# A four-direction scan layer: 32x32 tiles for gates, input and output products, gathered in one block per pair

## The chip, the core and the metric

The kernel runs on one core of a Trainium2 chip. The metric is the device time of one execution in microseconds (us), the median of several runs; lower is better. The core has five engines that run side by side and wait for each other by semaphores: PE (TensorE, matmuls; its weight loads are listed as PEld), DVE (VectorE), ACT (ScalarE), POOL (GpSimd) and SP (SyncE, here the queue that issues DMAs). [...] 

[...] All data are float32, and each float32 matmul of the program appears in the profile as two passes (two MATMUL records with a weight load each), so the profile has 24,090 records for 12,047 products.

## What is computed

The input x is (4, 128, 96, 96). It is normalized over groups of 4 channels (32 groups), run through the same layer in four scan orders (by rows, by rows backwards, by columns, by columns backwards), the four results are joined by a 1x1 product (fuse), and x is added.

```python
t = _grouped1x1(x, in_proj_w, in_proj_b, G)          # 128 -> 512 channels, 4 groups of 32
u, gate = (t[:, :HID], t[:, HID:])                   # HID = 256
u = jax.nn.silu(u)
u = conv_general_dilated(u, dw_w, ...)               # 5 taps, one filter per channel
s = _conv1x1(u, ssm_in_w)                            # 256 -> 32
a = DMIN + (DMAX - DMIN) * sigmoid(_conv1x1(u, ssm_delta_w, ssm_delta_b))
bb = tanh(_conv1x1(u, ssm_b_w, ssm_b_b)); cc = tanh(_conv1x1(u, ssm_c_w, ssm_c_b))
hst = scan of h = a * h + bb * s                     # written with cumsums in the reference
u = u + _conv1x1(cc * hst + ssm_d[None, :, None] * s, ssm_out_w)
u = _grouped1x1(u * sigmoid(gate), mix_w, mix_b, G)
return _conv1x1(u, out_proj_w, out_proj_b)
```

## The kernel before

**Tiling.** A batch element has two phases, V (columns) and H (rows); each phase treats its forward and backward order together (s = 0 and 1). A phase has NS = 6 steps of 16 lines, a step has R = 4 pairs; pair t holds the two units 2t (s = 0) and 2t + 1 (s = 1), each N = 384 positions wide (every fourth position of the step). That makes 8 phases, NP = 24 pairs a phase, 192 pairs in all; k = t % 4 is the place in the step. Because the backward order of one half of the lines is the forward order of the other, only the first three steps of a phase are computed up to the activations ("fresh"); the rest reads them mirrored, kept in DRAM meanwhile (`kept_sil`, and `kept` for gates). Gates belong to pair n = t - LAG (LAG = 6): the pair t works on the convolution and projection of its own units and, six pairs behind, on gate, output and final product of pair n. `mirror(n)` is None for the first 12 of 24, whose gates are computed.

**One pair.** The order on every engine is that of the program text (a manual schedule); `pair(t)` writes it out:
- in_proj of group g for the step after (`front`, L407 to L484; only while that step is fresh, t % 24 in 20 to 23 and 0 to 7): 16 products of 32x32 into four banks, then four silus on ACT (L470).
- the convolution of the first 128 channels on PE: `conv` (8 products, 128 x 32, "band") and `conv_less` (8 products, 64 x 32, "less", row half changing with s, column with g), copied to `u` by ACT (L629, L631). The other 128 channels on DVE: `first_tap` on ACT (L648), four taps on DVE (L650), in banks 0 and 1.
- W, the final product of two units gated in the pair before (`accumulate`, L742; 16 products, 128 x 32, "w_fin", to two banks), copied by ACT to `ys` (L755, L757) and added to `acc` by POOL (L774).
- `under` (L509): ACT seeds the output banks (0 and 1 for s = 0, 2 and 3 for s = 1) with u, so that the output product adds to it.
- gates (`gate`, L487; four products of 32x128, for pairs whose gates are computed) and outputs (`out_of`, L501; four products of 32x128), tanh of the gates on ACT (L521), and `gating` on DVE (L597), which multiplies.
- `proj` (L662): 16 products, 128 x 32, weights "main", to two banks; ACT evacuates them (L687, L688, L693), POOL forms decay and input of the scan (L695, L696).
- for k < 2 half of the scan of the step before on DVE (L722), and `outputs` on POOL (L728 to L731), which need it and feed the output product of a later pair.

The pairs differ: 10 of 24 have in_proj and outputs, 10 gates and outputs, two all three (t % 24 = 6, 7), two outputs alone (18, 19). PSUM banks 4 to 7 serve conv, W, in_proj, gates and proj in turn (`plan`, `GATE`, L121 to L127). The group norm of the next batch element is made in pieces (`stats_finish`, a generator; each `yield` ends a piece) between the pairs.

Of the kernel before, what the change touches and what calls it, by code (L numbers as in the profile page):

```python
# [67 lines left out]
def conv_preact_kernel(  # L68
# [111 lines left out]
    def stats_finish(b):  # L180

        mv = sp.tile([P, 2], F32, tag="mv", name=f"mv_{b}")
# [5 lines left out]
        nc.vector.tensor_copy(mean, pm[:, 0:1])  # L193
        dev = sp.tile([P, 1], F32, tag="dev", name=f"dev_{b}")
# [12 lines left out]
        nc.vector.tensor_scalar_add(var, pv[:, 0:2], GN_EPS)  # L207
        inv = sp.tile([P, 2], F32, tag="inv", name=f"inv_{b}")
        if b == b0:
            std = sp.tile([P, 2], F32, tag="err", name="std")  # L210
            nc.scalar.activation(std, var, AF.Sqrt)

            nc.scalar.activation(first_table, std[:, 0:1], AF.Silu)
            nc.vector.reciprocal(inv, std)
        else:
            bits = inv.bitcast(I32)
            nc.vector.tensor_single_scalar(bits, var.bitcast(I32), 1, ALU.logical_shift_right)
            nc.vector.tensor_scalar(bits, bits, -1.0, float(0x5F3759DF), ALU.mult, ALU.add)
            err = sp.tile([P, 2], F32, tag="err", name=f"err_{b}")
            for turn in range(3):  # L220
                if turn:
                    yield
                nc.gpsimd.tensor_mul(err, inv, inv)
# [3 lines left out]
        yield  # L227
        wns = sp.tile([P, 2, P], F32, tag="wn", name=f"wn_{b}")
        for e in range(2):
            nc.vector.tensor_scalar_mul(wns[:, e, :], w_in[:, e, :], inv[:, e : e + 1])  # L230
        wn = wns[:, 0, :]

        bn = sp.tile([P, 8], F32, tag="bnorm", name=f"bnorm_{b}")
        stats[b] = (wns, bn)
        yield


        pb = bank(free[0])
        product(pb[:, 0:4], wn, gm4)
        if b == b0:  # L240
            for g in range(4):
                for q in range(R):
                    mm(pb[:, 4 + g : 5 + g], q, wn[0:32, 32 * g : 32 * g + 32], mean[0:32, :], True, True)
            nc.vector.tensor_sub(bn, b_in, pb[:, 0:8])
        else:
            nc.vector.tensor_sub(bn[:, 0:4], b_in[:, 0:4], pb[:, 0:4])
            spread = sp.tile([P, 4], F32, tag="spread", name=f"spread_{b}")
            shift = sp.tile([P, 1], F32, tag="shift", name=f"shift_{b}")
            nc.vector.tensor_copy(shift, pb[:, 0:1])
            nc.vector.tensor_scalar_mul(spread, gmask, shift)  # L250
# [4 lines left out]
            nc.vector.tensor_sub(bn[:, 4:8], b_in[:, 4:8], pq[:, 0:4])  # L255
        nc.vector.tensor_scalar_mul(bn[:, 2:4], bn[:, 2:4], 0.5)


# [35 lines left out]
    def load_x(chunks):  # L294
        for c, n in chunks:
            nc.sync.dma_start(accf[:, bass.ds(c * SC, n * SC)], xr[b0, :, bass.ds(c * SC, n * SC)])  # L296
            for e in range(c, c + n):
                nc.vector.bn_stats(stats_of(b0)[:, e, :], accf[:, bass.ts(e, SC)])

    b0 = phases[0][0]  # L300
    mid = wp.tile([P, 1], F32, name="mid")
    nc.gpsimd.memset(mid, MID)
# [5 lines left out]
    w_out_fuse = load(fuse, "fuse")  # L308
    w_main = load(main, "main")
    for s in range(2):  # L310
        load_front(0, s, half(s), slice(0, R))
# [8 lines left out]
    w_mix = w_out_fuse[:, HID + 4 * P :].rearrange("p (j c) -> p j c", j=2)  # L320
    w_in, w_proj = (
        w_main[:, bass.ts(e, HID)].rearrange("p (j c) -> p j c", j=2) for e in range(2)
    )
# [135 lines left out]
            )  # L459

    def in_proj(step, g, s, j, bk):
        wn = stats[units[step * UB]["b"]][0]
        r = slice(64 * s + 32 * j, 64 * s + 32 * j + 32)
        for c in range(4):
            m, q = (c, g) if j else (g, R - 1 - c if s else c)
            mm(bank(bk), c, wn[r, s, 32 * m : 32 * m + 32], x_in[s][r, q, :], True, True)

    def silu(step, g, s, j, bk):
        bn = stats[units[step * UB]["b"]][1]
        nc.scalar.activation(  # L470
            sils[step][:, s, j, g, :],
            bank(bk)[:, : N + 1],
            AF.Silu,
            bias=bn[:, 1:2] if j else bn[:, 4 + g : 5 + g],
        )
# [11 lines left out]
    def gate(bi, s, j, to):  # L487
# [3 lines left out]
        nc.tensor.matmul(bank(to)[:, :N], stats[un["b"]][0][r, s, :], x_in[s][r, q, off : off + N],  # L491
                         start=True, stop=True)

    turning = (6, 0, 2)

    def ssm(bi, s):
# [4 lines left out]
    def out_of(bi, s, j):  # L501
# [2 lines left out]
        nc.tensor.matmul(bank(ssm(bi, s) + j)[:, :N], w_so[r, bass.ts(j, P)], z[r, :],  # L504
                         start=bi not in seeded, stop=True, skip_group_check=True)

    seeded = set()

    def under(bi, s):  # L509

        seeded.add(bi)
        nc.scalar.copy(psum[:, ssm(bi, s) : ssm(bi, s) + 2, :N], us[bi][:, s])  # L512

    def sigmoids(bi, to):
        bn = stats[units[bi]["b"]][1]
# [66 lines left out]
    def gating(bi, s):  # L582
# [1 line left out]
        v = units[bi + s]["v"] = us[bi][:, s]  # L584
        m = mirror(bi // 2)
        if m is None:
            g = gates[bi // 2 % 2][:, s]
        else:
            g = old_gates.get(bi // 2, gates[m % 2])[:, 1 - s, :, ::-1]
# [29 lines left out]
    def conv_less(i, banks):  # L619
# [7 lines left out]
        if banks == PROJ:  # L627
            for s in range(2):
                nc.scalar.copy(us[i][:, s, 0, :], bank(b0 + s)[:, :N])  # L629
# [167 lines left out]
    def pair(t):  # L797
# [124 lines left out]
        if bi > 0 and bi % (NU // B) == 0:  # L922
            send()

    def tail():

        first, end = NU // 2 - LAG, NU // 2
# [86 lines left out]
                nc.sync.dma_start(out[bu["b"], :, region], accf[:, region])  # L1014

    def start():
        w_of = wp.tile([P, 4, 2, P], F32, name="w_of")
# [93 lines left out]
    with tc.manual_schedule(  # L1111
# [2 lines left out]
        }  # L1114
    ):
        start()
        for t in range(NU // 2):
            pair(t)
        tail()


# [79 lines left out]
```

## Time and profile before

| what | us |
|---|---|
| three timed runs | 1810.45, 1811.15, 1817.87 |
| their median | 1811.15 |
| profiled execution, span from first to last instruction (its own time; none beside the span is listed) | 1812.7 |
| from the projection of pair 7 to that of pair 191 (184 pairs) | 1689.8 |

The profile names, for each engine, its busy time in the span, the chain of work that ended last (followed back from the last instruction to what released each step), groups of equal instructions with their mean duration, what each engine waited for, and the instructions in order of time. A row such as "914.09 0.88 PE L134 MATMUL psum<-sil,less 64*32 64x384 f32 x16" reads: from 914.09 us on, for 0.88 us, PE ran 16 passes of line 134, which read tiles sil and less with weights of 64 rows and 32 columns, and wrote to PSUM. "[0.16 <-PE psum L134]" behind a row is the time the engine stood idle before it, and whose end released it. L134 is the helper `mm`, so its rows are told apart by their tiles. PE's busy time overlaps itself, as matmuls are pipelined; the time from the start of one group to the start of the next is what a group takes.

### The profile page before, as it was taken

What the parts mean: (1) busy time and instruction counts of PE and PEld (TensorE: products, weight loads), DVE (VectorE), ACT (ScalarE), POOL (GpSimd) and SP (SyncE); (2) the same over time, 40 slices, a digit from 0 to 9 for tenths busy, and PEclk for the clock granted to TensorE, in tenths of its full rate; (3) what the DMA queues carried; (4) which work ended last, traced back from release to release, by engine and by line L of the source; (5) the groups of instructions that cost most, each with busy time, mean ns of one, the idle gap of its engine ahead of it and who ended that gap; (6) DMA issues with size and microseconds to landing.
All of it is one profiled execution on the core that took longest, in us unless ns stands there. A gap on an engine that the chain in (4) does not pass through costs nothing.

```text
span 1812.7 us, 56970 instructions
## 1 busy us (share of the span) xinstructions
PE 1788.9 (99%) x24090; PEld 645.3 (36%) x24090; DVE 1446.5 (80%) x1462; ACT 1567.0 (86%) x2750; POOL 1432.0 (79%) x1477
## 2 busy tenths in 40 slices
PE   6999999999999999999999999999999999999998
PEld 3333333333333333333333333333333333333333
DVE  5888878887888887877788888787877878777886
ACT  4988888998888888898988888889888888889975
POOL 3587887778778888788877888778778788887876
PEclk9999999999999999999999999999999999999999
DMA  7655463444975466344696447443477734645434
GB/s 229 183 184 196 149 185 117 163 145 142 305 246 188 159 177 204 102 145 141 204 306 225 159 161 211 138 146 119 160 232 223 249 118 150 192 122 176 148 112 175
DMA packets 148047, 321.17 MB, mean 177 GB/s; under 512 B 14160, under 2 KB 115920, under 8 KB 147792
## 3 DMA queue, kind: packets, MB, share of 16 engines
q1 hardware_dynamic: 147648, 317.48, 54.4%
q8 instruction: 190, 3.11, 0.7%
q14 instruction: 65, 0.53, 0.1%
q10 hardware_dynamic: 144, 0.04, 0.0%
HBM read 185.21 MB, written 132.25 MB: 175 GB/s over the span
## 4 chain that ended last, share of the span: by engine, by line
PE 95%; DMA 2%; DVE 2%; ACT 1%; issue 0%; SPq 0%; DVEq 0%
PE psum L134 82%; PE psum L504 8%; PE psum L491 5%; DVE psum L650 1%; DMA x_in<-in_xs 1%; DMA xs<-in_xr 1%; DMA acc<-in_xr 0%; DVE u L597 0%; DVE u L650 0%; ACT psum L512 0%; PE psum L1035 0%; ACT u L631 0%; SPq L296 0%; ACT ys L757 0%; DVE bn L387 0%
## 5 line engine op out<-in xcount | busy, mean ns | idle before, releaser
L650 DVE SCALAR_TENSOR_TENSOR psum<-sil,small,psum 128x768 f32<-128x768 f32 x576 | 589.0, 1023 | 28.4 <-ACT psum L648 3.4
L597 DVE SCALAR_TENSOR_TENSOR u<-gate,psum 128x768 f32<-128x768 f32 x376 | 350.0, 953 | 273.4 <-ACT u L629 119.0
L134 PE MATMUL psum<-u,w_fin 128*32 128x384 f32 (+1 forms) x6192 | 551.1, 485 | 1.6 <-ACT ys L755 1.2
L134 PE MATMUL psum<-u,main 128*32 128x384 f32 x6144 | 534.7, 489 | 1.5 <-DVE u L650 1.4
L774 POOL TENSOR_TENSOR acc<-ys,acc 128x384 f32<-128x384 f32 x375 | 411.6, 1119 | 24.0 <-ACT ys L757 7.9
L728 POOL TENSOR_TENSOR t<-t,t 64x384 f32<-64x384 f32 (+1 forms) x192 | 237.7, 1238 | 156.9 <-DVE t L722 73.2
L134 PEld LDWEIGHTS psum<-u,w_fin 128*32 128x32 f32 x6192 | 189.3, 109 | 319.6 <-issue 215.3
L134 PEld LDWEIGHTS psum<-u,main 128*32 128x32 f32 x6144 | 181.9, 109 | 324.7 <-issue 197.2
L512 ACT COPY psum<-u 128x768 f32<-128x768 f32 x352 | 277.3, 801 | 17.5 <-DVE u L650 11.5
L134 PE MATMUL psum<-sil,band 128*32 128x384 f32 x3072 | 285.1, 488 | 0.0
L695 POOL TENSOR_SCALAR t<-tm 64x384 f32<-64x384 f32 x191 | 176.9, 926 | 117.3 <-ACT tm L687 97.9
L729 POOL TENSOR_TENSOR t<-t,t 64x384 f32<-64x384 f32 (+1 forms) x192 | 249.1, 1297 | 15.0
L504 PE MATMUL psum<-t,main 32*128 32x384 f32 x1536 | 238.6, 513 | 1.3 <-ACT psum L512 0.6
L648 ACT ACTIVATE psum<-sil,small 128x768 f32<-128x768 f32 x191 | 173.7, 909 | 56.2 <-DVE u L597 48.0
L521 ACT ACTIVATE gate<-psum,bnorm 128x384 f32<-128x384 f32 x384 | 192.2, 584 | 26.5 <-PE psum L491 25.5
L696 POOL TENSOR_TENSOR t<-t,tm 64x384 f32<-64x384 f32 x192 | 195.3, 1017 | 15.3
L650 DVE SCALAR_TENSOR_TENSOR u<-sil,small,psum 128x768 f32<-128x768 f32 x192 | 194.9, 1015 | 7.8
L470 ACT ACTIVATE sil<-psum,bnorm 128x385 f32<-128x385 f32 x384 | 192.6, 585 | 7.1 <-PE psum L134 4.8
L134 PE MATMUL psum<-sil,less 64*32 64x384 f32 x3072 | 168.1, 495 | 0.0
L491 PE MATMUL psum<-x_in,wn 32*128 32x384 f32 x768 | 157.3, 527 | 0.0
L134 PEld LDWEIGHTS psum<-sil,band 128*32 128x32 f32 x3072 | 90.6, 109 | 169.2 <-issue 94.4
L731 POOL COPY t<-t 64x384 f32<-64x384 f32 x187 | 136.8, 731 | 11.9
(103 smaller groups left out, 1480.3 us busy)
## 6 DMA issues: line engine op xcount, KB each, us to landing
sil<-sil SPq DMA_DIRECT2D x128, 770.0 KB, 6.7
kept<-gate SPq DMA_DIRECT2D x80, 768.0 KB, 3.7
gate<-kept SPq DMA_DIRECT2D x76, 768.0 KB, 4.9
x_in<-in_xs SPq DMA_DIRECT2D x192, 96.2 KB, 2.5
out<-acc SPq DMA_DIRECT2D x48, 384.0 KB, 8.2
acc<-in_xr SPq DMA_DIRECT2D x39, 384.0 KB, 6.8
xs<-in_xr SPq DMA_DIRECT2D x72, 192.0 KB, 5.7
x_in<-in_xs SPq DMA_DIRECT2D x46, 192.5 KB, 3.5
```

The source lines that it names most:

```text
L134: nc.tensor.matmul(o[r, : rhs.shape[-1]], lhsT, rhs, start=start, stop=stop, skip_group_check=True)
L470: nc.scalar.activation(sils[step][:, s, j, g, :], bank(bk)[:, : N + 1], AF.Silu, bias=bn[:, 1:2] if j else bn[:, 4 + g : 5 + g],)
L491: nc.tensor.matmul(bank(to)[:, :N], stats[un["b"]][0][r, s, :], x_in[s][r, q, off : off + N], start=True, stop=True)
L504: nc.tensor.matmul(bank(ssm(bi, s) + j)[:, :N], w_so[r, bass.ts(j, P)], z[r, :], start=bi not in seeded, stop=True, skip_group_check=True)
L512: nc.scalar.copy(psum[:, ssm(bi, s) : ssm(bi, s) + 2, :N], us[bi][:, s])
L521: nc.scalar.activation(gv[:, s, j, :], bank(to[2 * s + j])[:, :N], AF.Tanh, bias=bn[:, 2 + j : 3 + j], scale=0.5,)
L597: nc.vector.scalar_tensor_tensor(v, g, 1.0, pz, ALU.add, ALU.mult)
L650: nc.vector.scalar_tensor_tensor(us[i][:, :, 1, :] if k == K - 1 else part, src, w_tap[:, k : k + 1], part, ALU.mult, ALU.add,)
L696: nc.gpsimd.tensor_mul(ta[0:64, p, :], tb[0:64, :], tm[0:64, :])
L728: engine.tensor_mul(ta[0:64, p, r], tb[64:P, r], ta[64:P, p, r])
L729: engine.tensor_add(tb[0:64, r], ta[0:64, p, r], tb[0:64, r])
L774: adder.tensor_add(part, y, part)
```

## The change

The pairs from t = LAG + 2 = 8 on go to a new function, `pair_of_tiles`, instead of `pair`. In it:
- gates and output products are split into four products of 32x32 (`gate_tile`, `out_tile`); in_proj has that shape already. One block of 32 products per pair holds 16 output products and 16 others: in_proj in the pairs that had it; otherwise gates of the pair n + 1 (one pair ahead of their use); in t % 24 = 17, 18, 19, where neither is left, the gates of the first three pairs of the next phase, which go through one tile `shared` to DRAM and come back later. The row group runs fastest, then the column. The block comes in two halves (j = 1, then 0): the first writes banks `pb` and 0, 1, the second `ob` and 2, 3.
- silu and tanh of the first half are one per bank, those of the second half one over two banks.
- order on PE: for k > 1 W, conv, less, block, proj; for k < 2 conv, less, W, block, proj. in_proj, which stood first in the pair, now stands in the block behind them. For k > 1 one of the two conv copies is DVE's.
- banks 6, 7 and 4, 5 change places from pair to pair; both output banks are always seeded.
- `stats_finish` is cut into smaller pieces, two of which run in each pair with k > 1.
- the weights of the start (`w_out_fuse`, `w_of`) lie in the tile `shared`, which is free after the start.

In numbers of instructions in the program (PE: products): 12,047 become 15,383; gates and outputs of 32x128 fall from 384 and 768 to 8 and 32, those of 32x32 rise from 0 to 1,504 and 2,944. ACT: silus 384 become 216 and 84 over two banks, tanhs 384 become 194 and 95, seeds 352 become 380, conv copies 178 and 103 (two banks) become 102 and 95, with 92 on DVE. Additions of u on DVE (L596) fall from 32 to 4. Gate loads from DRAM rise from 76 to 97; gate stores stay 80.

```diff
+    def gate_tile(n, s, j, to, c):
+        un = units[2 * n + s]
+        q, off = gate_at(un)
+        r = slice(64 * (1 - s) + 32 * j, 64 * (1 - s) + 32 * j + 32)
+        mm(bank(to), c, stats[un["b"]][0][r, s, bass.ts(c, 32)], x_in[s][r, q, off : off + N],
+           True, True)
...
+    def out_tile(bi, s, j, c):
+        r = slice(64 * j + 32 * s, 64 * j + 32 * s + 32)
+        mm(bank(ssm(bi, s) + j), c, w_so[r, bass.ds(j * P + 32 * c, 32)], tbs[bi][r, :], False, True)
...
+    def tanh_both(n, to, j, b0):
+        bn = stats[units[2 * n]["b"]][1]
+        nc.scalar.activation(
+            to[:, :, j, :],
+            psum[:, b0 : b0 + 2, :N],
+            AF.Tanh,
+            bias=bn[:, 2 + j : 3 + j],
+            scale=0.5,
+        )
...
+    def tile_of(n):
+        m = mirror(n)
+        return gates[((n % NP if m is None else m) + n // NP) % 2]
+
     def load_kept(n):
         m = mirror(n)
+        if n % NP < 3 and NP <= n < NU // 2:
+            nc.sync.dma_start(tile_of(n), kept[n // NP % 2][n % NP])
         if n < NU // 2 - R and m is not None and m < NP // 2 - 2:
-            old_gates[n] = gates[m % 2]
-            nc.sync.dma_start(old_gates[n], kept[n // NP % 2][m])
+            nc.sync.dma_start(tile_of(n), kept[n // NP % 2][m])
...
+    def less_both(i, banks):
+        step, p = units[i]["step"], units[i]["p"]
+        sil, k = blocks(step), less_of(p)
+        for g in range(4):
+            for s in range(2):
+                r = less_rows(s, p)
+                mm(bank(banks[s]), g, less[r, p, g, :], columns(step, sil[s][r, g, :], k), False, True)
...
+    def pair_of_tiles(t):
+        i, k, n, end = 2 * t, t % R, t - LAG, NU // 2
+        bi, last = 2 * n, t == end - 1
+        w_first = k > 1
+        pb, ob = ((6, 7), (4, 5))[:: 1 if t % 2 == 0 else -1]
+        cb, db = (ob, pb) if w_first else (pb, ob)
...
+        if mirror(n + 1) is None and (n + 1) % NP > 2:
+            gated = n + 1
+            to = tile_of(gated)
+        elif t % NP in (17, 18, 19) and t + LAG + 1 < end:
+            gated = t + LAG + 1
+            to = shared()[:, : 4 * N].rearrange("p (s j n) -> p s j n", s=2, j=2)
...
+        if t == LAG + 2:
+            for j in (1, 0):
+                b0 = pb[0] if j else SSM + 2
+                for c in range(4):
+                    for s in range(2):
+                        gate_tile(n, s, j, b0 + s, c)
+                tanh_both(n, tile_of(n), j, b0)
...
+        taps(i, (1, 2))
+        piece = later and k > 1
+        if piece:
+            free[0] = SSM + 2
+            next(later[0], None)
+        taps(i, (3, 4))
+        if piece:
+            next(later[0], None)
...
+        def convolution():
+            conv(i, cb)
+            if w_first:
+                under(bi, 0)
+            less_both(i, cb)
+            if w_first:
+                stats_chunks(t)
+                nc.scalar.copy(us[i][:, 0, 0, :], bank(cb[0])[:, :N])
+                nc.vector.tensor_copy(us[i][:, 1, 0, :], bank(cb[1])[:, :N])
+            else:
+                nc.scalar.copy(us[i][:, :, 0, :], psum[:, cb[0] : cb[0] + 2, :N])
+                under(bi, 0)
+                stats_chunks(t)
+
+        under(bi, 1)
+        if t > LAG + 2:
+            scale_s(i - 4)
+        if k < 2:
+            scan(t // R - 1, k)
+        if k != 1:
+            outputs(i - 10)
+        for part in (products, convolution) if w_first else (convolution, products):
+            part()
+        if k == 1:
+            outputs(i - 10)
...
+        for j in (1, 0):
+            for c in range(4):
+                for s in range(2):
+                    if fronted:
+                        in_proj_tile(step, g, s, j, (ob, pb)[j][s], c)
+                    elif gated is not None:
+                        gate_tile(gated, s, j, (ob, pb)[j][s], c)
+                for e in range(2):
+                    out_tile(bi, 1 - j, e, c)
+
+        if fronted:
+            for s in range(2):
+                silu(step, g, s, 1, pb[s])
+        elif gated is not None:
+            for s in range(2):
+                tanh_one(gated, to, s, 1, pb[s])
+        gating(bi, 0)
+        first_tap(i + 2)
+        gating(bi, 1)
+        if fronted:
+            silu_both(step, g, 0, ob[0])
...
+        elif gated is not None:
+            tanh_both(gated, to, 0, ob[0])
+            if gated % NP < NP // 2 - 2:
+                nc.sync.dma_start(kept[gated // NP % 2][gated % NP], to)
+            for s in range(2):
+                load_gate(2 * gated + s + UB)
...
+        proj(i, pb, True)
...
         start()
-        for t in range(NU // 2):
+        for t in range(LAG + 2):
             pair(t)
+        for t in range(LAG + 2, NU // 2):
+            pair_of_tiles(t)
         tail()
```

More of the change, by code (lines that the diff above doesn't have):

```diff
@@ L298, in load_x, with shared @@
                 nc.vector.bn_stats(stats_of(b0)[:, e, :], accf[:, bass.ts(e, SC)])
+    rp = ctx.enter_context(tc.tile_pool(name="shared", bufs=1))
+    def shared():
+        return rp.tile([P, 16 * P], F32, tag="shared", name="shared")
     b0 = phases[0][0]
@@ L307, in conv_preact_kernel @@
     load_x([(0, 1), (1, 1), (2, 1), (3, 2), (5, 2), (7, 3), (10, 4), (14, 4), (18, 4), (22, 2)])
-    w_out_fuse = load(fuse, "fuse")
+    w_out_fuse = shared()
+    nc.sync.dma_start(w_out_fuse[:, 0 : 2 * HID + 4 * P], fuse)
     w_main = load(main, "main")
@@ L461, in in_proj, with in_proj_tile @@
     def in_proj(step, g, s, j, bk):
+        for c in range(4):
+            in_proj_tile(step, g, s, j, bk, c)
+    def in_proj_tile(step, g, s, j, bk, c):
         wn = stats[units[step * UB]["b"]][0]
         r = slice(64 * s + 32 * j, 64 * s + 32 * j + 32)
-        for c in range(4):
-            m, q = (c, g) if j else (g, R - 1 - c if s else c)
-            mm(bank(bk), c, wn[r, s, 32 * m : 32 * m + 32], x_in[s][r, q, :], True, True)
+        m, q = (c, g) if j else (g, R - 1 - c if s else c)
+        mm(bank(bk), c, wn[r, s, 32 * m : 32 * m + 32], x_in[s][r, q, :], True, True)
     def silu(step, g, s, j, bk):
@@ L472, in silu, with silu_both @@
             bank(bk)[:, : N + 1],
+            AF.Silu,
+            bias=bn[:, 1:2] if j else bn[:, 4 + g : 5 + g],
+        )
+    def silu_both(step, g, j, b0):
+        bn = stats[units[step * UB]["b"]][1]
+        nc.scalar.activation(
+            sils[step][:, :, j, g, :],
+            psum[:, b0 : b0 + 2, : N + 1],
             AF.Silu,
@@ L586, in gating @@
         if m is None:
-            g = gates[bi // 2 % 2][:, s]
+            g = tile_of(bi // 2)[:, s]
         else:
-            g = old_gates.get(bi // 2, gates[m % 2])[:, 1 - s, :, ::-1]
+            g = old_gates.get(bi // 2, tile_of(bi // 2))[:, 1 - s, :, ::-1]
         pz = psum[:, ssm(bi, s) : ssm(bi, s) + 2, :N]
@@ L1016, in start @@
     def start():
-        w_of = wp.tile([P, 4, 2, P], F32, name="w_of")
         def filler(n):
```

79 lines of the change are left out of this document (78 added, 1 removed).

## The prediction

> **What bounds the kernel now.** I read the page's busy shares and its chain first, then the waits of PE, then PE's instructions in order of time, pair by pair.
>
> ```profile
> span 1812.7 us, 56970 instructions
> PE 1788.9 (99%) x24090; PEld 645.3 (36%) x24090; DVE 1446.5 (80%) x1462; ACT 1567.0 (86%) x2750; POOL 1432.0 (79%) x1477
> ...
> PE 95%; DMA 2%; DVE 2%; ACT 1%; issue 0%; SPq 0%; DVEq 0%
> ...
> PE psum L134 <- DVE u L650: 1.4, 2, 1.0
> ```
>
> PE makes 95% of the chain, and for L650, the taps on DVE, it waited 1.4 us in the whole run, the most for any engine behind the start's loads. So PE's stream sets the time, and the question is how long PE's steps take. Here are a pair with an in_proj (t = 97, k = 1), then one with gates; start, length, passes.
>
> ```profile
> 909.21 0.94 PE L134 MATMUL psum<-x_in,wn 32*32 32x385 f32 x32
> 910.09 1.50 PE L134 MATMUL psum<-sil,band 128*32 128x384 f32 x16
> 911.40 2.76 PE L134 MATMUL psum<-u,w_fin 128*32 128x384 f32 x32
> 914.09 0.88 PE L134 MATMUL psum<-sil,less 64*32 64x384 f32 x16
> 914.90 0.93 PE L504 MATMUL psum<-t,main 32*128 32x384 f32 x8
> 915.76 2.79 PE L134 MATMUL psum<-u,main 128*32 128x384 f32 x32
> 918.48 0.94 PE L134 MATMUL psum<-x_in,wn 32*32 32x385 f32 x32
> ...
> 603.66 2.79 PE L134 MATMUL psum<-u,main 128*32 128x384 f32 x32
> 606.27 1.47 PE L134 MATMUL psum<-sil,band 128*32 128x384 f32 x16
> 607.56 1.47 PE L134 MATMUL psum<-u,w_fin 128*32 128x384 f32 x16
> 608.96 0.88 PE L134 MATMUL psum<-sil,less 64*32 64x384 f32 x16
> 609.76 1.50 PE L134 MATMUL psum<-u,w_fin 128*32 128x384 f32 x16
> 611.19 0.59 PE L491 MATMUL psum<-x_in,wn 32*128 32x384 f32 x2
> ...
> 916.43 0.13 PEld L134 LDWEIGHTS psum<-u,main 128*32 128x32 f32 x4 [0.19 <-issue]
> 916.75 0.13 PEld L134 LDWEIGHTS psum<-u,main 128*32 128x32 f32 x4 [0.19 <-issue]
> ```
>
> From start to start the first pair is 918.48 - 909.21 = 9.27 us. The weight loads show the beat: four column tiles run together, a set of four passes every 916.75 - 916.43 = 0.32 us. I call that a wave. The 64-row tiles (less) run 8 to a wave and in_proj's 32x32 tiles 16: 32 passes are two waves, 0.64 us, of the 0.88 us up to conv at 910.09. The pair has 4 + 8 + 2 + 2 + 8 + 2 = 26 waves = 8.3 us; the other 0.9 us lies where the tile shape changes (five times; the same-shape step conv to W, 1.31 for four waves, loses almost nothing). The whole stretch that the new loop replaces runs from the projection of pair 7 to that of pair 191:
>
> ```profile
> 88.31 2.76 PE L134 MATMUL psum<-u,main 128*32 128x384 f32 x32
> 1778.10 2.79 PE L134 MATMUL psum<-u,main 128*32 128x384 f32 x32
> ```
>
> That is 1689.8 us for 184 pairs, 9.18 each.
>
> **The change, part by part.** Waves: a gate or output product of 32x128 becomes four of 32x32, so the counts of passes rise, but four row groups times four columns run together. A block has 16 + 16 products, 64 passes, four waves: the same as gates plus outputs, or in_proj plus outputs, had. Twelve in_proj pairs, nine gate pairs and three early-gate pairs per phase of 24 all have 26 waves; before it was 26 in 20 pairs, 28 in two, 24 in two: the same sum. So nothing is won on arithmetic; what is won are shape changes. They are now three in a pair with k > 1 (conv to less, less to block, block to projection) and four with k < 2.
>
> Does the order inside the block, with the row group running fastest, keep 16 together? The less products stand in that order (both row halves of a column, then the next column) and take 0.81 us for 16 passes, two waves of 8. I take full concurrency.
>
> The pair with k > 1: projection, W and conv are 80 passes of one shape. Rows: 603.66 to 608.96 is 5.30 for 64 of them with the change to less; 16 more at 607.56 - 606.27 = 1.29 give 6.59. Less to block 0.81 (914.09 to 914.90; the change from 64x32 to 32x32 itself isn't shown, less to W is 0.80, so I take 0.81). Block to projection: in_proj's 0.88 plus two more waves, 0.64, is 1.52 if nothing waits. Sum 8.92. With k < 2: projection and conv then less, 4.00 (48 passes after a change, 910.09 to 914.09); less to W 0.80; W to block 2.72 (915.76 to 918.48); block 1.52: 9.04. Mean 8.98, against 9.18.
>
> But the block now stands between two handoffs that must end inside it.
>
> ```profile
> 914.09 0.88 PE L134 MATMUL psum<-sil,less 64*32 64x384 f32 x16
> ...
> 915.06 0.86 ACT L629 COPY u<-psum 128x384 f32<-128x384 f32 x2 [0.16 <-PE psum L134]
> ...
> 915.95 1.82 DVE L597 SCALAR_TENSOR_TENSOR u<-gate,psum 128x768 f32<-128x768 f32 x2 [1.30 <-ACT u L629]
> ...
> 916.94 0.91 ACT L648 ACTIVATE psum<-sil,small 128x768 f32<-128x768 f32 x1 [0.51 <-DVE u L597]
> ...
> 602.26 0.48 ACT L757 COPY ys<-psum 128x384 f32<-128x384 f32 x1
> ...
> 602.79 0.18 PEld L491 LDWEIGHTS psum<-x_in,wn 32*128 32x128 f32 x1
> ...
> L470 ACT ACTIVATE sil<-psum,bnorm 128x385 f32<-128x385 f32 x384 | 192.6, 585 | 7.1 <-PE psum L134 4.8
> ...
> 910.45 2.00 ACT L470 ACTIVATE sil<-psum,bnorm 128x385 f32<-128x385 f32 x4
> ...
> L1031 DVE COPY w_of<-psum 128x256 f32<-128x256 f32 x1 | 0.4, 424 | 0.0
> L193 DVE COPY mean<-psum 128x1 f32<-128x1 f32 x4 | 0.6, 153 | 0.4 <-PE psum L134 0.4
> ```
>
> ACT starts 0.09 after less ends (914.97 to 915.06), and PE loads weights 0.05 after ACT's copy ends (602.74 to 602.79).
> 1. The projection writes its first bank where the first half's in_proj or gate result lies. That half ends like in_proj, 0.94 after the block's start; + 0.09, silu 0.585, + 0.05: 1.66.
> 2. The second half (k > 1) writes the conv banks, one of which DVE now copies. From less: 0.88 + 0.09 + the copy + 0.05. DVE's copy of 128x384 isn't in the trace: 0.42 at least (128x256), 0.91 at most (half of L597's 1.82, 768 elements each); from 1 to 256 elements it grows 1.06 ns each, so I take 0.56. That is 1.58, or 0.77 after the block's start, where two waves would allow 0.64; the other half then costs 0.88: 1.65.
> 3. With k < 2 the second half waits for ACT's copy of W's second bank. W ends 0.04 into the block (2.76 long, next step at 2.72); + 0.09 + 0.48 + 0.05 is 0.66, about when the first half's two waves are through.
>
> So block to projection is 1.65, not 1.52: 9.05 and 9.17. Sum over 92 pairs of each kind: 1676 us. Seven last pairs have outputs alone (0.88 in place of 1.65: -5.4), pair 8 makes two gates (+0.9, one in_proj's worth). 1671.7 against 1689.8 is -18.1 us. The start (w_of in a shared tile, same operations) and the tail stay.
>
> What costs nothing, and its cover: the merged silus and tanhs (two banks at once, 0.91 by L648 against 2 x 0.585 at worst) end 3.0 + 0.9 = 3.9 after the block's start, when conv or W needs their bank at 1.65 + 2.61 = 4.26; gone, each 0.1 is 18 us. The finer steps of the group norm, in pairs with k > 1, cover eight pairs and end before the early gates. The 21 more reloads of gates:
>
> ```profile
> gate<-kept SPq DMA_DIRECT2D x76, 768.0 KB, 4.9
> ...
> 906.50:915.80 9.30, 9.30 (x144) 3.17 (x143) 7.72 (x7) 8.37 (x16) 5.14 (x6) 1.00 1.04 315
> ...
> PE psum L134 <- DMA x_in<-in_xs: 0.4, 1, 0.4
> ```
>
> Each has two pairs, 18 us, for a landing of 4.9, though the engines are full (share 1.04) in some pairs near them; fully exposed it would be 21 x 4.9 = 103 us, and I take 0. On SP's queue behind them stand x_in and xs loads with a pair or more to spare; the 0.4 us is all PE ever waited for x_in here.
>
> [...]
>
> **The rivals.**
> - B, the handoffs hide: silu and copy end sooner by 0.13. For it: 0.94 counts to the last tile, the first bank is ready earlier. 92 x (8.92 + 9.04) - 7 x 0.64 + 0.9 = 1648.8: -41, so 1770.
> - C, the two halves don't overlap: the wait in the middle keeps the weights of the second half from being loaded ahead, so a block is two in_projs, 2 x 0.88 = 1.76. 92 x (9.16 + 9.28) - 7 x 0.88 + 0.9 = 1691: +1.4, so 1812.5. For it: PE's loads of a shape stand ahead of each wave. Against: 0.05 from release to load.
> - D, slower: ACT's queue arrives late in pairs with k < 2.
>
> ```profile
> 909.21 0.25 PEld L134 LDWEIGHTS psum<-x_in,wn 32*32 32x32 f32 x32 [0.62 <-issue]
> ...
> L512 ACT COPY psum<-u 128x768 f32<-128x768 f32 x352 | 277.3, 801 | 17.5 <-DVE u L650 11.5 <-DVE u L597 3.4
> ...
> L705 ACT ACTIVATE t<-t,small 64x384 f32<-64x384 f32 x192 | 118.8, 619 | 2.6
> L693 ACT ACTIVATE t<-psum,small 64x384 f32<-64x384 f32 x192 | 111.0, 578 | 4.9
> ...
> L688 ACT COPY t<-psum 64x384 f32<-64x384 f32 x192 | 91.0, 474 | 6.8
> ...
> L755 ACT ACTIVATE ys<-psum,b_fin 128x384 f32<-128x384 f32 x94 | 54.6, 581 | 16.6 <-PE psum L134 16.5
> ```
>
> Behind the projection's end (1.65 + 2.79 + 0.09 = 4.53 after the block's start) ACT has copy 0.47, tanh 0.58, seed 0.80, scale 0.62, conv copy 0.80 (of L512's size), seed 0.80, W copies 0.58 and 0.48: 5.13, to 9.66; the second half needs the last at 9.17 + 0.64 - 0.05 = 9.76. ACT's instructions overlap now (four silus in 2.00, not 4 x 0.585 = 2.34), worth 0.8 over these eight. If they lose that and each pays a 0.09 hop, the last is 9.66 + 0.72 - 9.76 = 0.62 late: 92 x 0.62 = +57, 1850. It decides once the eight take over 0.9 more than overlapped. Against: ACT is busy 8.37 us in the row of 906.50 and has its pairs of 9.27 in time; the 179 merges take 179 x 0.26 = 47 us off it and DVE's 92 copies 92 x 0.43 = 40, while 28 more seeds add 22.
> - E, slower still: passes cost a fixed time one after another. [...] Against: 32 weight loads in 0.25 us, and less's 0.81.
>
> That the merge doesn't happen is no rival: the built order shows 32 products in one run between less or W and the projection.
>
> **How the numbers follow.** The sum is made in the profiled execution, span 1812.7; the median of the runs is 1811.15, 1.5 lower, and I carry the difference over: 1811.15 - 18.1 = 1793. Chances: mine 0.42 (1783 to 1802), B 0.17, C 0.20, D 0.16, E 0.05. About 0.5% (9 us) is what a measurement of this kernel can tell from no change: below 1802 is faster, B and nearly all of mine, 0.58; C and the rest of mine give 0.21; slower 0.21. The range reaches from B to DVE's copy at its upper bound (0.35 more in 92 pairs, +32, 1825), a little beyond both: 1766 to 1829.
>
> **What would show it.** PE's rows: projection to projection 9.05 and 9.17 in turn, a block of 64 passes about 1.65 before the projection, weight loads in its middle released by DVE's or ACT's copy, those of the projection by ACT L491 or L557. Wrong: blocks of 1.5 (B), 1.76 or more (C), block starts waiting for ACT L553 or L825 (D), a DVE copy far from 0.56, gating that waits for gate<-kept.

## The result and the profile after

| | us |
|---|---|
| predicted | 1793 (1766 to 1829) |
| measured, median of 4 runs | 1863.37 (1860.28 to 1868.51) |
| before, on the same chip | 1811.14 |
| ratio | 1.029 (95% interval 1.026 to 1.031) |
| profiled execution, span | 1861.3 (before 1812.7) |

The change makes the kernel 2.9% slower; the forecast had the wrong sign. First the page of the changed kernel: busy times, the queue that carries instructions (packets, MB), the chain.

```profile
span 1861.3 us, 70398 instructions
...
PE 1825.1 (98%) x30762; PEld 681.7 (37%) x30762; DVE 1450.3 (78%) x1526; ACT 1535.3 (82%) x2515; POOL 1445.9 (78%) x1477
...
q8 instruction: 243, 3.98, 0.9%
...
PE 96%; DMA 1%; DVE 1%; issue 1%; ACT 1%; SPq 0%; DVEq 0%
```

PE is the bound as before, ACT and DVE aren't, and PE's passes rise from 24,090 to 30,762. Now PE's instructions in order of time, a pair with k > 1 (block at 1068.78), then the steps of one with k < 2.

```profile
1061.38 2.79 PE L134 MATMUL psum<-u,main 128*32 128x384 f32 x32
1063.99 2.76 PE L134 MATMUL psum<-u,w_fin 128*32 128x384 f32 x32
1066.57 1.47 PE L134 MATMUL psum<-sil,band 128*32 128x384 f32 x16
1067.97 0.88 PE L134 MATMUL psum<-sil,less 64*32 64x384 f32 x16
1068.78 0.51 PE L134 MATMUL psum<-x_in,wn 32*32 32x384 f32 x2
...
1069.26 0.52 PE L134 MATMUL psum<-t,main 32*32 32x384 f32 x2
1069.47 0.70 PE L134 MATMUL psum<-x_in,wn 32*32 32x384 f32 x2
1069.67 0.51 PE L134 MATMUL psum<-t,main 32*32 32x384 f32 x2
...
1070.68 2.79 PE L134 MATMUL psum<-u,main 128*32 128x384 f32 x32
...
1079.98 2.79 PE L134 MATMUL psum<-u,main 128*32 128x384 f32 x32
1082.58 1.47 PE L134 MATMUL psum<-sil,band 128*32 128x384 f32 x16
1083.99 0.88 PE L134 MATMUL psum<-sil,less 64*32 64x384 f32 x16
1084.79 2.79 PE L134 MATMUL psum<-u,w_fin 128*32 128x384 f32 x32
1087.51 0.51 PE L134 MATMUL psum<-x_in,wn 32*32 32x384 f32 x2
...
1089.41 2.79 PE L134 MATMUL psum<-u,main 128*32 128x384 f32 x32
```

Read start to start: 2.61 + 2.58 + 1.40 + 0.81 up to the block, then 1.90 to the projection: 9.30. With k < 2: 2.60 + 1.41 + 0.80 + 2.72, then 1.90: 9.43. Nearly all of the 177 pairs with a full block are like these. The copies that the second half waits for:

```profile
1068.94 0.48 ACT L1060 COPY u<-psum 128x384 f32<-128x384 f32 x1 [0.56 <-PE psum L134]
1069.84 1.05 ACT L557 ACTIVATE gate<-psum,bnorm 128x384 f32<-128x384 f32 x2 [0.43 <-PE psum L134]
...
1069.05 0.56 DVE L1061 COPY u<-psum 128x384 f32<-128x384 f32 x1 [1.28 <-PE psum L134]
```

DVE's copy takes the estimated 0.56, but starts 0.20 behind less (1068.85), not 0.09. It ends at 1069.61, and 0.06 later the rest of the second half runs. Read from this trace alone, the wait of the prediction's step 2 seems to be the cause, a bit later than costed. The experiments say otherwise.

Last, PE's waits behind its first, for the kernel's input (us in total, times, longest), and one of the places behind the largest of them:

```profile
PE psum L134 <- issue: 10.0, 5, 2.7
PE psum L134 <- ACT sil L500: 3.0, 1, 3.0
PE psum L134 <- DVE u L720: 2.7, 2, 2.2
PE psum L134 <- ACT gate L563: 1.8, 1, 1.8
...
514.79 0.84 PE L134 MATMUL psum<-u,main 128*32 128x384 f32 x5
...
518.01 1.60 PE L134 MATMUL psum<-u,main 128*32 128x384 f32 x12 [2.38 <-issue]
```

In the middle of a projection PE stops behind five passes and waits for nothing that the profile names. There are five such stops: 2.42 us from one pass to the next at 475.56, 2.87 at 515.14, 2.61 at 932.84, 3.17 at 1390.28 and 1.35 at 400.40. A sixth, 3.44 at 971.87, lies between a block and its projection. Less 0.08 that a pass of a projection takes anyway, and 0.41 for the change of shape at the sixth, that is 15.1 us (the expectations below count 15.4); before had none. For the sixth the list names a silu (L500, 3.0), but that ends at 974.32, and PE goes on only at 975.31; what the six share is told below, behind the run without the acc loads.

**Where the time went.** Against the sum, block to projection is 1.90 instead of 1.65, so pairs are 0.25 (k > 1) and 0.27 (k < 2) longer: 88 x 0.25 + 89 x 0.27 = +46. The pairs that stand out, those with stops and behind them and pair 8 (12.38), are 23.8 longer than the steady ones, 22.9 after the 0.9 expected for pair 8. (Pair 8 alone is 2.95 longer: at 91.13 PE has waited 1.8 for the tanh of the two gates that it makes first.) What lies outside the 184 pairs is 2.8 shorter. -18.1 + 46 + 22.9 - 2.8 = 48; measured 1861.3 - 1812.7 = 48.6.

### The profile page after: what moved, and what is told of

Same layout as the page of the kernel before. It is cut to its first block, busy times and chain, and to the rows that moved or that the text cites. A ratio compares the mean times of both kernels' runs of the same rounds, so it can differ in the third digit from the quotient of the medians.

```text
span 1861.3 us, 70398 instructions
## 1 busy us (share of the span) xinstructions
PE 1825.1 (98%) x30762; PEld 681.7 (37%) x30762; DVE 1450.3 (78%) x1526; ACT 1535.3 (82%) x2515; POOL 1445.9 (78%) x1477
## 3 DMA queue, kind: packets, MB, share of 16 engines
q8 instruction: 243, 3.98, 0.9%
## 4 chain that ended last, share of the span: by engine, by line
PE 96%; DMA 1%; DVE 1%; issue 1%; ACT 1%; SPq 0%; DVEq 0%
PE psum L134 95%; DMA xs<-in_xr 1%; DMA acc<-in_xr 0%; DVE bn L309 0%; PE psum L541 0%; DVE psum L720 0%; PE psum L521 0%; DVE u L659 0%; SPq L307 0%; PE psum L1237 0%; PE psum L1245 0%; ACT psum L553 0%; ACT t L775 0%; DVE bn L405 0%; ACT sil L491 0%
## 5 line engine op out<-in xcount | busy, mean ns | idle before, releaser
L134 PE MATMUL psum<-u,w_fin 128*32 128x384 f32 (+1 forms) x6192 | 533.7, 485 | 1.1 <-ACT ys L825 0.6
L659 DVE SCALAR_TENSOR_TENSOR u<-gate,psum 128x768 f32<-128x768 f32 x376 | 342.3, 951 | 180.1 <-PE psum L134 94.8
L134 PE MATMUL psum<-x_in,wn 32*32 32x385 f32 (+1 forms) x6080 | 354.9, 493 | 0.1
L134 PE MATMUL psum<-t,main 32*32 32x384 f32 x5888 | 354.0, 492 | 0.0
L553 ACT COPY psum<-u 128x768 f32<-128x768 f32 x380 | 307.2, 809 | 9.6 <-DVE u L659 3.8
L799 POOL TENSOR_TENSOR t<-t,t 64x384 f32<-64x384 f32 (+1 forms) x192 | 297.5, 1549 | 15.1
L798 POOL TENSOR_TENSOR t<-t,t 64x384 f32<-64x384 f32 (+1 forms) x192 | 234.7, 1222 | 19.4 <-DVE t L792 5.0
L766 POOL TENSOR_TENSOR t<-t,tm 64x384 f32<-64x384 f32 x192 | 199.9, 1041 | 16.7 <-ACT t L758 1.4
L134 PEld LDWEIGHTS psum<-x_in,wn 32*32 32x32 f32 x6080 | 139.2, 103 | 192.8 <-ACT psum L553 55.0
L1061 DVE COPY u<-psum 128x384 f32<-128x384 f32 x92 | 51.3, 558 | 156.2 <-PE psum L134 156.2
L134 PEld LDWEIGHTS psum<-sil,band 128*32 128x32 f32 x3072 | 100.8, 110 | 153.6 <-issue 96.1
L827 ACT COPY ys<-psum 128x384 f32<-128x384 f32 x281 | 129.9, 480 | 28.6 <-PE psum L134 27.3
```

The lines of the kernel that those rows point to most:

```text
L134: nc.tensor.matmul(o[r, : rhs.shape[-1]], lhsT, rhs, start=start, stop=stop, skip_group_check=True)
L659: nc.vector.scalar_tensor_tensor(v, g, 1.0, pz, ALU.add, ALU.mult)
L766: nc.gpsimd.tensor_mul(ta[0:64, p, :], tb[0:64, :], tm[0:64, :])
L798: engine.tensor_mul(ta[0:64, p, r], tb[64:P, r], ta[64:P, p, r])
L799: engine.tensor_add(tb[0:64, r], ta[0:64, p, r], tb[0:64, r])
L827: nc.scalar.copy(ys, y)
```

## The experiments

Two things had to be found: why 64 passes take 1.90, and what the stops are.

**Outputs ahead in the second half.**

```diff
         for j in (1, 0):
+            if not j:
+                for c in range(4):
+                    for e in range(2):
+                        out_tile(bi, 1, e, c)
             for c in range(4):
...
-                for e in range(2):
-                    out_tile(bi, 1 - j, e, c)
+                if j:
+                    for e in range(2):
+                        out_tile(bi, 0, e, c)
```

> Of the changed kernel, the second half of the block with its 8 output products ahead of its 8 in_proj or gate products (they stood in turn); nothing else. Theory LATE (the second half's in_proj or gate products wait for the copy of the bank they write, until about 0.88 us after the block's start, and hold back the output products queued behind them): the outputs no longer wait, the waiting products are 16 passes that start at 0.88, so block to projection is about 0.88 + 0.32 + 0.13 + 0.41 = 1.74 instead of 1.90, 177 times 0.16 = 28 us less: 1835 (1826 to 1844). Rival SPLIT (64 passes of 32x32 cost 1.90 by their number, whatever their order): block to projection stays 1.90, 1863 (1858 to 1868).

1863.16 us, ratio to before 1.028 (1.026 to 1.030): no change. PE's rows of this kernel, end of a block:

```profile
1073.34 0.51 PE L134 MATMUL psum<-x_in,wn 32*32 32x384 f32 x2
...
1073.83 0.98 PE L134 MATMUL psum<-t,main 32*32 32x384 f32 x10
...
1074.67 0.65 PE L134 MATMUL psum<-x_in,wn 32*32 32x384 f32 x8
1075.25 2.79 PE L134 MATMUL psum<-u,main 128*32 128x384 f32 x32
```

1073.34 to 1075.25 is 1.91. LATE falls: the waiting products stand last now, and nothing is won. The wait is moved here, not taken away. Copies that read a constant, so that the second half waits for no bank, would take it away, but leave two products that write one bank in no order; such a kernel has no time.

**The kernel before, only split.** Gates and outputs as four 32x32 products each, in the old places.

```diff
-        nc.tensor.matmul(bank(ssm(bi, s) + j)[:, :N], w_so[r, bass.ts(j, P)], z[r, :],
-                         start=bi not in seeded, stop=True, skip_group_check=True)
+        for c in range(4):
+            mm(bank(ssm(bi, s) + j), c, w_so[r, bass.ds(j * P + 32 * c, 32)], z[r, :],
+               bi not in seeded, True)
```

> The kernel before, with each gate and output product of 32x128 as four of 32x32 at the place where it stood; order, banks and waits stay. If splitting by itself is what costs (SPLIT, half of the block's 0.38 us over the ideal for each 32 passes, in 192 output groups and 96 gate groups): 288 x 0.19 = +55, 1866 (1845 to 1880). If it costs nothing (LATE): 1811 (1803 to 1818), plus what FETCH adds by the larger number of instructions alone, at most 15: up to 1826.

1852.34 us, 1.023 (1.021 to 1.024), 41 more than before. So splitting costs by itself, with the old waits and banks. A pair with gates and one with outputs behind in_proj:

```profile
1040.34 0.55 PE L134 MATMUL psum<-x_in,wn 32*32 32x384 f32 x8
...
1041.78 0.53 PE L134 MATMUL psum<-x_in,wn 32*32 32x384 f32 x4
1042.24 2.79 PE L134 MATMUL psum<-u,main 128*32 128x384 f32 x32
...
935.49 1.01 PE L134 MATMUL psum<-t,main 32*32 32x384 f32 x32
936.43 2.79 PE L134 MATMUL psum<-u,main 128*32 128x384 f32 x32
```

64 passes of gates and outputs take 1.90 here too (16 wide ones took 1.58 before, the median of 80 such pairs), while 32 passes of outputs take 0.94 (8 wide ones 0.86). It isn't half of the loss for each 32 passes, as SPLIT had it: the second 32 cost far more than the first. The single matmul records show it; medians of all such runs, us behind the run's first pass:

| run | count | pass 17 | 32 | 33 | 34 | 64 | next shape |
|---|---|---|---|---|---|---|---|
| before, in_proj, 32 passes | 93 | 0.35 | 0.46 | | | | 0.875 |
| changed kernel, block | 177 | 0.35 | 0.47 | 0.69 | 0.88 | 1.49 | 1.905 |
| outputs ahead, block | 177 | 0.35 | 0.47 | 0.68 | 0.86 | 1.49 | 1.905 |
| split in place, gates and outputs | 96 | 0.35 | 0.46 | 0.70 | 0.86 | 1.49 | 1.903 |

In the three kernels with 64 passes, whatever their order, operands and waits, the 34th pass starts 0.86 to 0.88 behind the first (in no block of the changed kernel sooner than 0.864), and from there passes come mostly 16.7 ns apart, with some pauses (up to there mostly 6.7). The copies' wait makes 0.02 of it (0.88 against 0.86). The next shape starts 0.41 behind the last pass in every row, and 0.41 to 0.42, in the median, at the other changes between such shapes here: the change costs what I had taken.

**Wide gates.** The split undone in the pairs without in_proj: two gates of 32x128, four outputs, two gates.

```diff
+        if not fronted:
+            gate_wide(1)
+            for s in range(2):
+                for e in range(2):
+                    out_of(bi, s, e)
+            gate_wide(0)
-        for j in (1, 0):
+        for j in (1, 0) if fronted else ():
```

> Of the changed kernel, with the split undone in the pairs without in_proj: gates and outputs are 32x128 products again there (16 passes instead of 64), at the same place, with two gates ahead of the outputs and two behind them; banks, copies and the order of all else stay. Theory RUN (a block costs 1.90 because it is one run of 64 passes, and no wait sets it): block to projection falls to 1.50 to 1.58 there (the old gate block has 1.58), 92 pairs by 0.32 to 0.40: -29 to -37, and up to 10 less for stops of PE with a fifth fewer instructions: 1825 (1814 to 1836). Rival LATE (the copies of conv or W set it): 1.90 stays there, 1863 (1855 to 1868).

1832.98 us, 1.012 (1.010 to 1.015): 30 less than the changed kernel, as RUN has it. A block with k < 2:

```profile
1063.29 0.59 PE L521 MATMUL psum<-x_in,wn 32*128 32x384 f32 x2
...
1064.38 0.48 PE L521 MATMUL psum<-x_in,wn 32*128 32x384 f32 x2
1064.87 2.79 PE L134 MATMUL psum<-u,main 128*32 128x384 f32 x32
```

1.58 there, but 1.72 with k > 1 (1044.92 to 1046.64): without the stop the wait for the conv copies, of which DVE's ends at 1045.75 there, seems to show, at 0.14. No run takes that wait alone away, so this is likely and not shown.

**Wide wherever possible.** In the pairs with in_proj, too, outputs and one half of in_proj are wide; 8 products of 32x32 remain.

```diff
+                elif fronted and j:
+                    r = slice(64 * s + 32, 64 * s + 64)
+                    nc.tensor.matmul(bank(pb[s])[:, : N + 1],
+                                     stats[units[step * UB]["b"]][0][r, s, :], x_in[s][r, g, :],
+                                     start=True, stop=True)
```

> As with the wide gates, and in the pairs with in_proj too every product that can be wide is wide: outputs 32x128, the half of in_proj with one input for all columns (j = 1) as two products of 32x128, and behind the outputs the other half as 8 products of 32x32, 16 passes. Theory RUN: no run of 32x32 has over 16 passes now; wide part 0.64 + 0.1 + 0.41 = 1.15, then 0.19 + 0.41 = 0.60, so block to projection 1.75 in these pairs instead of 1.90, 84 x 0.15 = 13 us under the 1833 of the wide gates: 1820 (1812 to 1828), a little less if PE stops less often for its instructions. Rival SHAPE (the change from 32x128 to 32x32 costs as much as the stop behind 33 passes did): 1.90 or more there, 1833 to 1845.

1854.08 us, 1.023 (1.021 to 1.026): longer, as SHAPE said, and by more, but not for its reason. A block:

```profile
1152.48 0.59 PE L1087 MATMUL psum<-x_in,wn 32*128 32x385 f32 x2
...
1153.97 0.88 PE L134 MATMUL psum<-x_in,wn 32*32 32x385 f32 x16
1154.78 2.79 PE L134 MATMUL psum<-u,main 128*32 128x384 f32 x32
```

1.49 + 0.81 = 2.30. The change from wide to 32x32 costs 0.41 like the others (median of 84), so RUN was sized wrong in both parts. The 12 wide passes start in four sets (0, 0.43, 0.75 and 1.07) and take 1.49 where I had reckoned 1.15. The 16 passes of 32x32 go 8 and 8, one row group 0.35 behind the other, and take 0.81 where I had reckoned 0.60. That two row groups don't start together here, as they do in in_proj of the kernel before (16 passes there, the 17th 0.35 behind the first), stays unexplained. So in the pairs with in_proj the split block, 1.90, is the better of the two.

**What the stop counts.** Four kernels. First, longer runs:

```diff
+        again = (t // R) % 4
+        for j in ((), (0,), (1, 0), (1, 0, 1, 0))[again]:
+            for c in range(4):
```

> Of the changed kernel, with in_proj or gate products of the block done again behind it, into the same banks with the same values: no product again in the pairs with (t // 4) % 4 = 0, 8 products for 1, 16 for 2, 32 for 3, so that runs of 64, 80, 96 and 128 passes of 32x32 stand side by side in one execution. In the blocks of the split kernel the 34th pass starts 0.86 us after the first, in whatever order the products stand. Theory ONCE (one stop behind 33 passes, from there 16 passes each 0.33): the last pass starts 1.49, 1.82, 2.15 and 2.81 after the first. Rival EACH (the stop comes again every 32 passes, which cost 1.02 then): 1.49, 1.85, 2.51 and 3.53. The time of the whole only tells the added passes.

The last pass came 1.49, 2.18, 2.31 and 3.15 behind the first (k > 1): neither theory. The repeated products use two row groups at a time, not four, which I hadn't allowed for; this one is inconclusive.

Then the outputs last:

```diff
-                for e in range(2):
-                    out_tile(bi, 1 - j, e, c)
+        for s in range(2):
+            for c in range(4):
+                for e in range(2):
+                    out_tile(bi, s, e, c)
```

> Of the changed kernel, the block's products in another order: both halves of in_proj or gates first, then all 16 outputs. So the wait for the copies comes at the 17th and 18th pass and not at the 33rd. Theory TIME (the 34th pass can't start before 0.86 us behind the run's first, however the time went by): the 18th starts at 0.885, and nothing stops behind the 33rd, waves of 16 passes go on each 0.33, the last pass at about 1.7, block to projection 2.1: +0.2 in 177 pairs, 1900 (1890 to 1910). Rival COUNT (the stop of 0.17 comes behind 33 passes whenever they ran): 2.3, 1930 (1915 to 1945).

1985.68 us, 1.096 (1.093 to 1.099), blocks of 2.37 to 2.61: both sizes are wrong. The 16 products of in_proj or gates use two row groups in turn, column by column, and go 8 passes each 0.35 us, which neither theory had. Nothing stops at the 33rd pass; it comes at 1.0 or later, when 0.86 is past.

```diff
-        for j in (1, 0):
+        for j in (0, 1):
             for c in range(4):
```

> Of the changed kernel, the halves of the block in the other order: the half whose in_proj or gate products wait for the copies comes first, so that nearly all of its 64 passes are held until about 0.69 and 0.88 us (k > 1) behind the end of less, and PE stands with the whole run queued. COUNT (the 34th pass stops behind the 33rd whenever the run gets going): the 34th starts 0.17 behind the 33rd again, about 0.86 after the pass that was released last, block to projection some 0.85 longer than 1.90, 2.75. CLOCK (the stop is a matter of time since the shape changed, and a wait covers it): the 34th follows the 33rd without a gap, 0.2 less, 2.5. The whole: 1863 + 177 x 0.85 = 2013 or 1978, each by 20.

2096.58 us, one run. With k < 2 the first two passes start 0.35 apart, the third 0.67 behind the first. From there they go in sets (from 0.67, 1.02 and 1.34) up to the 34th at 1.35, and the 35th starts at 1.53: 0.18 behind it, 32 passes and 0.86 us behind the third. With k > 1 the second starts at 0.19, and the 35th, again 0.18 behind the 34th, at 1.06: 0.86 behind the second. So COUNT holds for the stop: it comes again once the run gets going. The size is wrong: the projection now also waits for the silu or tanh of the half that comes last (53.5 us of waits for ACT's copies, 52.5 and 44.8 for silu and tanh).

Last, 8 tiny products, so that passes and work differ:

```diff
                     if fronted:
+                        if j:
+                            in_proj_tile(step, g, s, j, pb[s], c, 1)
                         in_proj_tile(step, g, s, j, (ob, pb)[j][s], c)
```

> Of the changed kernel, with 8 tiny products added to the first half of the block: ahead of each in_proj or gate product of j = 1 the same product for one column alone (16 passes of 32x32x1, which write what is written again behind them). Theory QUEUE (what stops is the supply of instructions: some 33 passes, each with its weight load, stand ready when the run gets going, and the next come 0.86 later): the stop comes behind the 33rd pass of the run, tiny ones counted, the 34th still starts at about 0.86, but only 17 full passes are done by then, so the other 47 end at 0.86 + 47/16 x 0.33 = 1.83, block to projection 2.24 instead of 1.90: 1863 + 177 x 0.34 = 1923 (1905 to 1940). Rival TILE (the stop comes where a tile is used for the second time, with the third set of 16 full passes): the tiny passes only take their own time, 16 of at most 16.7 ns, the stop stands behind the 33rd full pass, the 49th of the run, and block to projection is 1.90 to 2.17 with a 34th pass at about 0.36 to 0.4: 1863 to 1910.

2004.21 us, one run; blocks of 2.71. The largest gap of a block lies behind the 35th pass, 0.60 to 0.92 behind the first (medians of 177), tiny ones counted, 12 of the 35 being tiny; behind the 49th there is none of that kind. That is QUEUE's place and not TILE's: the stop comes by the number of passes here, not by their work; what holds PE there no trace shows. Its size was off here too, as the rest then goes slower than 16 passes in 0.33: in the block at 1102.49 the 45 passes behind the stop start within 1.37, from 1103.41 to 1104.78.

**The stops in mid-projection.** First the early gates' loads left out:

```diff
-        if n % NP < 3 and NP <= n < NU // 2:
-            nc.sync.dma_start(tile_of(n), kept[n // NP % 2][n % NP])
```

> Of the changed kernel, without the 21 loads of the early gates from DRAM (n % 24 < 3), so that these pairs are gated with an older gate; nothing else. Theory FETCH (six stops of PE in mid-projection, 15.4 us in sum, come from PE's own instructions being loaded late, as that load stands behind data transfers, and the 21 loads crowd just these places): the stops at 475, 515, 933 and 1390 us get shorter or vanish, 1848 (1846 to 1856). Rival COUNT (PE simply has 28% more instructions, and the loads have no part in it): the stops stay, 1863 (1859 to 1868).

1865.18 us, 1.029 (1.026 to 1.033): no change. In its profile the stops at 515 and 933 are gone, those near 400, 475, 965 and 1383 are there, some longer, 11.0 us in sum. The time is COUNT's. The four runs go from 1857 to 1871, so the 21 loads cost nothing that can be measured.

Then the loads of x into acc left out:

```diff
-            for b, r in reload:
-                nc.sync.dma_start(accf[:, r], xr[b, :, r])
             reload.clear()
```

> Of the changed kernel, without the loads of the next batch's x into acc (four of 384 KB at a time, which stand where the DMA engines are full), so that x isn't added and acc isn't started anew behind the first batch element. Theory FETCH (PE's stops in mid-projection are its own instructions coming late behind data): the stops near 400, 475, 515, 933, 972 and 1390 us go, 15 us: 1848 (1843 to 1856). Rival: they stand at places in PE's stream that have nothing to do with the traffic, and stay: 1863 (1857 to 1869).

1854.30 us, 1.023 (1.021 to 1.026): 9 less. Three stops of six are left (510, 925 and 966 us), 7.7 us instead of 15.1. The time fits FETCH, which had all six gone; half of them went.

What the stops have in common is read from the DMA packets of the queue q8 "instruction": 16 KB each, one for every 126.6 passes (30,762 / 243; 126.2 to 127.1 in all eight profiles of the table, so the loads go with PE's passes). Take for each load how far PE was, at its landing, past 126.6 passes for every load before it (what PE held ahead of the first load isn't known, so only differences count).

| kernel | loads | past 200 | stops |
|---|---|---|---|
| before | 190 | none, latest 180 | none |
| changed | 243 | six, 206 to 222 | six, 15.1 us |
| outputs ahead | 243 | six, 206 to 222 | six, 14.9 us |
| split in place | 244 | two, 206 and 209 | two, 2.7 us |
| without the gates' loads | 243 | five, 206 to 219 | four, 11.0 us |
| without the acc loads | 243 | three, 210 to 217 | three, 7.7 us |
| wide gates | 207 | three at 223 and 224, four at 204 to 213 | three, by the first three, 9.3 us |
| wide wherever possible | 183 | none, latest 179 | none |

At each of these 24 stops PE goes on 1.2 to 1.6 us behind the landing of such a load. That holds for the sixth of the changed kernel, too: its load lands at 973.97 and PE goes on at 975.31, 0.99 behind the end of the silu. I read it so that PE stops where its own next instructions land late; no profile names that wait. What speaks for it is that the two fall together in these profiles, and that traffic taken away took half of the stops with it (15.1 us became 7.7); what delays just these loads I didn't settle.

## Why the prediction was wrong

- "Projection, W and conv ... 6.59", "less to block 0.81", 4.00, 0.80 and 2.72: measured 6.59, 0.81, 4.01, 0.80 and 2.72. Counting shape changes was right, and so was the cost of each.
- "Block to projection: in_proj's 0.88 plus two more waves, 0.64, is 1.52 if nothing waits" is the step that failed. The third and fourth wave cost 1.905 - 0.875 = 1.03. I took "full concurrency" from less, a run of 16 passes, and the price from in_proj, a run of 32; I carried the rate past the longest run that I had read, and gave it no bounds. The trace of before has one longer run, 128 passes at its start, 32 of them of one column: it waits for its input and then takes 5.34 us for 88 passes (24.34 to 29.68). It is no steady run, but it was no support for the rate either.
- The handoffs (steps 1 to 3), on which rival B and the block's 1.65 rested, didn't set the time. DVE's copy was sized right (0.56), its start 0.11 too early; moving it out of the way gained nothing. The tanh of the first half ends 1.64 behind the block's start (1069.84 + 0.58), about as reckoned, with the projection 0.26 later.
- Rival C came nearest with its 1.76, for another reason: not the wait in the middle separates the halves, but a stop behind the 33rd pass, the 34th starting at 0.88 with that wait in the middle and at 0.86 with it 16 passes later. D didn't come, and that its 1850 lies near the measured time is chance: but for the stop at 971.87, the waits for ACT in PE's list are 1.8 us or less each. E, passes that cost a fixed time one after another, would be +183 us, 0.0275 a pass (in_proj's 0.88 for 32) for all 6,672. Splitting alone cost 41 us for 3,456 more products, 12 ns each, and unevenly: 32 passes in a row took 0.94 in place of 0.86, 64 took 1.90 in place of 1.58.
- "What costs nothing": the reloads did cost nothing that can be measured, as the run without them says. Put at nothing without a reason was the loading of the program itself: queue q8 brought 243 packets of instructions in place of 190, 28% more, and the row on full engines (share 1.04), which I read for the gates alone, may bear on that. The stops are 15.1 us. Pair 8 was put at 0.9 and took 2.95.

Of the other waits in the list above, the 2.7 us for DVE lie at 41.09 and 55.01, ahead of the changed pairs (before has 1.4 for the same taps), and the 1.8 is pair 8's. No kernel here beats the one before.

## What to carry over

Before a rate is carried to a longer run of small matmuls, look for a run that long in a trace, or measure one: here a run of 32 passes of 32x32 took 0.88 us, the change of shape behind it included, and one of 64 took 1.90, more than two runs of 32. Where a trace shows a wait at the place of a loss, move the wait alone before believing it. And more instructions on the bounding engine were also more bytes to load here: 3.98 MB in place of 3.11, 28% more, came with 15.1 us of stops, and half of them went with other traffic.

## What was not expected of the hardware

- In the three kernels of the table with 64 passes, 33 passes of 32x32 go without that stop, and the 34th starts 0.86 to 0.88 us behind the first. With the waiting half first, the pass that starts 0.86 behind the second or third is the 35th; with tiny products the 36th starts 0.92 behind the first. Why it takes 0.86 stays open.
- How many passes start together hangs on the order. 16 do (the 17th starts at 0.35) where four row groups of two columns, or, in in_proj of the kernel before, the four columns of one row group and then of another, follow each other; two row groups in turn, column by column, gave 8 each 0.35 us, and so did the last 16 passes of the kernel with everything wide. No rule that covers all of these was found.
- By the records, PE starts passes out of the program's order. In the kernel with the outputs last, where every output stands behind all 16 products of in_proj or gates, one output pass starts ahead of seven of theirs:

```profile
1147.65 1.52 PE L134 MATMUL psum<-x_in,wn 32*32 32x384 f32 x25
1148.87 0.48 PE L134 MATMUL psum<-t,main 32*32 32x384 f32 x1
1148.88 0.53 PE L134 MATMUL psum<-x_in,wn 32*32 32x384 f32 x7
1149.01 1.32 PE L134 MATMUL psum<-t,main 32*32 32x384 f32 x31
```
